# First unit's second maxima settled one step earlier, third unit's q and k projected later, in a fused attention kernel

## The chip, the cores and the metric

The kernel runs on one core of a Trainium2 chip. Such a core has a matrix engine (TensorE, PE in the profile; its weight loads are PEld), a vector engine (VectorE, DVE), an activation engine (ScalarE, ACT), a general engine (GpSimd, POOL) and a small engine that here only starts transfers (SyncE, SP). They run side by side and wait for one another through semaphores. Transfers run on 16 DMA engines. A time is the device time of one execution in microseconds; of several runs the median is given.

## The reference

A mixture-of-experts block, causal attention, and the same mixture-of-experts block again, each added to its input, for x of 8 batches x 1024 tokens x 256 features:

```python
x = x + 0.5 * _L0_ffn_ref(_layernorm(x), ...)
x = x + _L0_attn_ref(_layernorm(x), Wq, bq, Wkv, bkv, Wo, bo)
x = x + 0.5 * _L0_ffn_ref(_layernorm(x), ...)
...
dots = jnp.einsum('bhid,bhjd->bhij', q * scale, k)
dots = jnp.where(causal, MASK_VAL, dots)
attn = jax.nn.softmax(dots, axis=-1)
out = jnp.einsum('bhij,bhjd->bhid', attn, v)
```

There are 16 heads of 16 features. An expert that more than 1280 of the 16384 choices (two for each token) fall to is dropped with all its tokens. The kernel counts the choices and runs the expert code only if some expert stays under that bound; with these inputs only the attention and the two counts run.

## The kernel before

`attention` (L684) works in 32 **units**: a unit u is one batch (b = u // 4) and one group of four heads (g = u % 4). For a unit there are four kinds of work.

- **Projection**, `project(u)` (L821): two halves of 512 tokens. A half is 16 matmuls into a tile pq, a copy with bias into `packed` on ACT, and eight transfers of 32 KB (L845) that spread the heads over the rows of kT and qT, all on SP's queue except those of the first unit's k. kT and qT have four buffers each, used in turn.
- **Maxima**, `m_steps(u)` (L851): 24 steps of score blocks (tile `sm`) whose row maxima DVE takes, with the causal mask where it applies, into the columns of `top0` (queries 0 to 511) and `top1` (queries 512 to 1023).
- **Settling**, `settle(u, hf)` (L885): DVE turns `top` (a 32x32 transpose, tile `turned`), SP sends it to memory (L889, `top_d`), and three steps later fetches it back (L891) as a 17th row of each head of qT. The matching row of kT is -1, so that the scores of the next kind of work come out less their maximum.
- **Scores and values**, `e_steps(u)` (L897): 24 steps. Score blocks come out transposed (tile `sc`), ACT takes their exponential (`pT`), POOL masks the diagonal, and matmuls with v (`vaug`) add up in `pav`. Steps 0 to 7 are queries 0 to 511, steps 8 to 23 the others. The first sc of steps 8 on needs the row of `settle(u, 1)`.

The main loop (L1211) takes the scores and values of unit u together with the maxima of unit u + 1, step by step. It begins with u = -1, where only unit 0's maxima are there. From step 14 of u = -1 on, the first eight score steps of unit 0 run beside them. So in u = 0 steps 0 to 7 have maxima of unit 1 alone (in pairs, at even steps), and steps 8 to 23 have both.

The six score tiles (L698) take turns, `sm` and `sc` alike, and a second pool of two banks (L702) serves pq, pv, px, pav and the rest.

Everything else is fed in by a small planner, `Beside` (L53). A piece of work is a generator: it yields a number (go on in so many steps), PIECE or QK (go on when a step offers that kind), or REST (the second part of a piece just begun: it goes on in the next step). `step(kinds)` first runs all that is due by its number, then one piece of an offered kind. `finish` runs a work to its end at once. At the start of u = 0 the planner holds the values of batch 0's last tiles (`values_of`, tile pv), the remaining weight preparation (`turning`: pt_w, then g_mean and gcs on DVE, pt_gc, pg, pb_v), the residual of batch 0, `project(2)`, whose kind is QK, and `prepare(1, ...)` (L730), which loads batch 1 and later takes its layer-norm statistics, one tile of 128 tokens at a time, on DVE. `prepare` must be done by unit 1's step 7.

PE, DVE, ACT and POOL keep the order in which the program names their work; SP's order comes from the scheduler that builds the kernel.

All engine instructions go through one helper, so the profile shows line 37 for nearly all of them: tiles tell them apart. Transfers carry their own lines.

Of the kernel before, what the change touches and what calls it, by code (L numbers as in the profile page):

```python
# [49 lines left out]
PIECE, QK, REST = "piece", "qk", "rest"  # L50
# [53 lines left out]
def macaron_kernel(  # L104
# [210 lines left out]
    def ln_stats(xb, j, st, mv):  # L315
        vector.bn_stats(st[:, j, :], xb[:, j, :D])
        vector.bn_aggr(mv[:, j, :], st[:, j, :])

    def ln_tiles(what):
        st = norm.tile([P, TB, 6], F32, tag="st", name=f"st_{what}")  # L320
        mv = norm.tile([P, TB, 2], F32, tag="mv", name=f"mv_{what}")
        return st, mv

    def ln_rstd(mv, what, std=None):
        n = mv.shape[1]
        ve = norm.tile([P, TB], F32, tag="ve", name=f"ve_{what}")
        gpsimd.tensor_scalar(ve[:, :n], mv[:, :, 1], EPS, None, ALU.add)
        rstd = norm.tile([P, TB], F32, tag="rstd", name=f"rstd_{what}")
        gpsimd.tensor_tensor(rstd[:, :n], ve[:, :n], half[:, :n], ALU.pow)
        if std is not None:  # L330
            gpsimd.tensor_tensor(std, ve[:, :n], rstd[:, :n], ALU.mult)
        return rstd
# [351 lines left out]
    def attention(run_no, src, dst, gate0, logits, tally):  # L684
# [3 lines left out]
        with stack:  # L688
# [41 lines left out]
            def prepare(b, wait, apart):  # L730
                xb = xbs[b] = ap.tile([P, TB, D + E], F32, tag="xa", name=f"xa{b}", bufs=3)
                nc.sync.dma_start(out=xb[:, :, :D], in_=src[b].rearrange("(j p) d -> p j d", p=P))
                yield wait
                st, mv = ln_tiles(f"a{b}")
                for j in range(TB):
                    ln_stats(xb, j, st, mv)
                    yield apart
                stds[b] = norm.tile([P, TB], F32, tag="std", name=f"std{b}")
                lns[b] = mv, ln_rstd(mv, f"a{b}", stds[b])
                yield 2  # L740
# [62 lines left out]
            def residual(b):  # L803
                xb, lg = xbs[b], lgs.pop(b)
                gpsimd.tensor_tensor(
                    xb[:, :, D:], lg, stds.pop(b).unsqueeze(2).to_broadcast([P, TB, E]), ALU.mult
                )
                for j in range(0, TB, 2):
                    part = xb[:, j : j + 2, :]
                    gpsimd.tensor_tensor(part, part, bo_all.unsqueeze(1).to_broadcast([P, 2, D + E]), ALU.add)  # L810
                    yield 2
# [9 lines left out]
            def project(u, parts=(0, 512)):  # L821
                b, g = divmod(u, NG)
                xnT = xnTs[b]
                for s0 in parts:
                    yield QK
                    pq = bank(f"pq{u}_{s0}")
                    for c in range(DC):
                        matmul_cols(
                            pq,
                            wkqT[:, c, g].rearrange("p a d -> p (a d)"),  # L830
                            xnT[:, c, s0 : s0 + 512],
                            start=(c == 0),
                            stop=(c == DC - 1),
                        )
                        if c + 1 < DC:
                            yield REST
                    packed = ap.tile([P, 512], F32, tag="packed", name=f"packed{u}_{s0}", bufs=4)
                    scalar.activation(packed, pq, AF.Identity, bias=bkqT[:, g : g + 1], scale=1.0)
                    if u > 3:

                        nc.sync.dma_start(out=qTs[u % 4][HD::32, s0 : s0 + 512], in_=zeros)
                    for k in range(8):
                        r = 32 * (k % 4)

                        (nc.scalar if u == 0 and k < 4 else nc.sync).dma_start(  # L845
                            out=(kTs, qTs)[k // 4][u % 4][r : r + HD, s0 : s0 + 512],
                            in_=packed[HD * k : HD * (k + 1), :],
                        )
# [36 lines left out]
            def settle(u, hf):  # L885
                turned = ap.tile([P, 32], F32, tag="turned", name=f"turned{u}_{hf}")
                vector.transpose(turned, tops[hf])
                top_d = spill.tile([32, 4, 32], F32, tag="top_d", name=f"top_d{run_no}_{u}_{hf}", bufs=3)
                nc.sync.dma_start(out=top_d.rearrange("c b p -> b c p"), in_=turned)  # L889
                yield 3  # L890
                nc.sync.dma_start(  # L891
                    out=qTs[u % 4][HD::32, hf * 512 : hf * 512 + 512],
                    in_=top_d[:16].rearrange("(h i) b p -> h (i b p)", h=4),
                )
# [308 lines left out]
            beside = Beside()  # L1203
# [7 lines left out]
            for u in range(-1, NU):  # L1211
                b, g = divmod(u, NG)
                if u == 0:
                    beside.finish(opening)
                    preparing = beside.add(prepare(1, 2, 2))
                    projecting = beside.add(project(2))
                    beside.add(chain((PIECE,), turning, residual(0)))
                if u >= 0 and g == 2 and b + 1 < B:
# [9 lines left out]
                if g == 3 and u >= 0:  # L1228
                    if b + 2 < B:
                        preparing = beside.add(prepare(b + 2, STEPS + 8, 1))  # L1230
# [5 lines left out]
                def step(k, e):  # L1236


                    scores, then = es[e]
                    for h in range(2):  # L1240
                        scores(h)
                        if ms[k] is not None:
                            ms[k](h)
                    now = u * STEPS + k
                    if then is not None:
                        owed.append((now + 2, then, 0))
                        owed.append((now + 3, then, 1))
                    while owed and owed[0][0] <= now:
                        _, then, part = owed.popleft()
                        then(part)  # L1250
# [4 lines left out]
                for k in range(STEPS) if u < 0 else range(8) if u == 0 else ():  # L1255
                    if u < 0 and 14 <= k < 22:
                        step(k, k - 14)
                    elif k % 2 == 0:
                        for h in range(2):
                            ms[k](h)  # L1260
                            ms[k + 1](h)
                    if u < 0 and k == 7:
                        beside.add(settle(0, 0), first=True)
                        for kT in kTs[2:]:
                            scalar.copy(kT, row16.to_broadcast([P, S]))
                    if u == 0 and k == 1:
                        while owed:
                            _, then, part = owed.popleft()
                            then(part)
                        settling = beside.add(settle(0, 1), first=True)  # L1270
                    if u == 0 and k == 7:
                        beside.finish(settling)
                    beside.step((QK, PIECE) if u == 0 or not 14 <= k < 20 else ())
                for k in range(0, STEPS, 2) if u == NU - 1 else ():

                    then = es[k + 1][1]
# [21 lines left out]
                for k in range(0 if u else 8, STEPS) if 0 <= u < NU - 1 else ():  # L1298
# [30 lines left out]
                    if k == 0:  # L1329
                        settling = beside.add(settle(u, 1), first=True)  # L1330
# [30 lines left out]
    logits = [route.tile([P, NT, E], F32, name=f"logits{k}") for k in range(2)]  # L1361
    tallies = [tally_tile("0"), tally_tile("1")]
    leasts = attention(0, x, out, (logits[0], tallies[0]), logits[1], tallies[1])
    some0 = kept("0", leasts[0])
    either = route.tile([P, 1], I32, name="either")
    vector.scalar_tensor_tensor(either, leasts[1], float(CAP), some0, ALU.is_le, ALU.max)
    with tc.If(branch_on(either) > 0):
        some1 = kept("1", leasts[1])

        with tc.If(flag(some0, "0") > 0):  # L1370
            feed_forward(0, logits[0], x, xw_d)
            tally = tally_tile("1b")
            anew = attention(1, xw_d, out, None, logits[1], tally)
            vector.tensor_copy(some1, kept("1b", anew[1]))
        with tc.If(flag(some1, "1") > 0):
            feed_forward(1, logits[1], out, out)
# [40 lines left out]
```

## Time and profile before

| | us |
|---|---|
| median of 3 runs (lowest, highest) | 1357.85 (1356.86, 1359.06) |
| the profiled execution | 1351.15 |
| its span, first to last instruction | 1349.4 |
| idle time of TensorE before an `sc` that waited for qT<-top_d | 8.6 |
| mean granted TensorE clock, share of full | 0.989 |

Beside these, 40 equal slices of the span are shown on the page as digits: the busy tenths of each engine and the clock granted to TensorE.

```profile
PE   6799999999999999999999999999999999999994
PEld 2233333333333333333333333333333333333331
DVE  6766677778777787877778777777787777877865
...
PEclk9999999999999999999999999999999999999997
```

A slice is 33.7 us; the second one (33.7 to 67.5) is where the change is, and PE has a 7 there. A stall of some microseconds is visible only in a finer view: the list of waits (who waited, for whom, how long in total, how often, the longest), the chain of work that ended last with start times, the timeline of one engine, or the busy time of the engines in chosen stretches.

### The profile page before, as it was taken

The numbers are of one execution on the slowest core, as the hardware profiler recorded it, in microseconds if no ns is written. First come the engines' busy times: TensorE is split into PE (matmuls) and PEld (weight loads), VectorE is DVE, ScalarE is ACT, GpSimd is POOL, SyncE is SP. The second block draws the span as 40 slices with busy tenths as digits, with TensorE's granted clock in tenths as the row PEclk, the third lists the DMA queues.
The fourth block names the chain that finished last, engine by engine and source line by source line (L and its number), as shares of the span: only waits on it lengthen the run. The fifth ranks groups of instructions, "written<-read, shape, count | busy, mean of one in ns | idle before, by whom it ended". The sixth has DMA issues, their size and how long they took to land.

```text
span 1349.4 us, 51518 instructions
## 1 busy us (share of the span) xinstructions
PE 1309.2 (97%) x20664; PEld 436.6 (32%) x20664; DVE 1016.4 (75%) x3299; ACT 806.7 (60%) x1908; POOL 439.8 (33%) x776
## 2 busy tenths in 40 slices
PE   6799999999999999999999999999999999999994
PEld 2233333333333333333333333333333333333331
DVE  6766677778777787877778777777787777877865
ACT  3346666566666665666666666656566666666562
POOL 3134113542146221452125521354214621143321
PEclk9999999999999999999999999999999999999997
DMA  4101112112211121222122221211221111122201
GB/s 146 41 4 43 43 39 61 58 47 69 59 54 57 53 62 49 61 59 59 51 59 61 58 75 38 62 57 52 65 61 55 55 53 32 48 60 60 64 24 34
DMA packets 67024, 73.73 MB, mean 55 GB/s; under 512 B 24688, under 2 KB 42232, under 8 KB 66776
## 3 DMA queue, kind: packets, MB, share of 16 engines
q1 hardware_dynamic: 65432, 69.56, 17.7%
q8 instruction: 165, 2.70, 0.8%
q10 hardware_dynamic: 1344, 0.79, 0.2%
q14 instruction: 83, 0.68, 0.2%
HBM read 26.87 MB, written 26.20 MB: 39 GB/s over the span
## 4 chain that ended last, share of the span: by engine, by line
PE 94%; DVE 3%; DMA 1%; SPq 1%; issue 1%; ACT 0%; POOL 0%; ACTq 0%; DVEq 0%
PE sc L37 42%; PE pav L37 24%; PE pq L37 8%; PE sm L37 8%; PE pv L37 4%; PE px L37 4%; PE pta L37 1%; SPq L845 1%; DVE first L37 1%; DMA xa<-in_L_attn_x_dram 0%; PE px_last L37 0%; DVE st_g L37 0%; DVE cand_g L37 0%; DVE xa L37 0%; POOL rstd_g L37 0%
## 5 line engine op out<-in xcount | busy, mean ns | idle before, releaser
L37 ACT ACTIVATE pT<-sc 128x512 f32<-128x512 f32 (+3 forms) x1536 | 669.0, 488 | 469.8 <-PE sm L37 353.7
L37 PE MATMUL sm<-kT,qT 32*64 32x512 f32 (+3 forms) x6144 | 726.9, 507 | 0.0
L37 PE MATMUL sc<-qT,kT 32*64 32x512 f32 (+3 forms) x6144 | 695.1, 507 | 8.6 <-DMA qT<-top_d 8.6
L37 POOL TENSOR_SCALAR_AFFINE_SELECT pT<-pT 128x256 f32<-128x256 f32 x512 | 207.6, 407 | 772.6 <-ACT pT L37 765.0
L37 DVE TENSOR_REDUCE first<-sm 128x1 f32<-128x512 f32 x512 | 328.3, 684 | 82.2 <-PE sm L37 66.7
L37 PE MATMUL pav<-pT,vaug 128*32 128x160 f32 (+4 forms) x5120 | 381.9, 370 | 2.8 <-POOL pT L37 2.0
L37 DVE CUSTOM_DVE_ANT_0 sm<-sm,causal 128x256 f32<-128x256 f32 (+3 forms) x512 | 242.2, 516 | 117.9 <-PE sm L37 110.1
L37 DVE CUSTOM_DVE_ANT_0 sm<-sm,causal,first 128x256 f32<-128x256 f32 (+3 forms) x512 | 262.3, 557 | 86.1 <-PE sm L37 74.1
L37 PEld LDWEIGHTS sc<-qT,kT 32*64 32x64 f32 x6144 | 184.3, 130 | 376.9 <-ACT pT L37 303.7
L37 PEld LDWEIGHTS pav<-pT,vaug 128*32 128x32 f32 x5120 | 102.4, 108 | 363.1 <-issue 268.3
L37 PEld LDWEIGHTS sm<-kT,qT 32*64 32x64 f32 x6144 | 203.3, 130 | 14.2 <-issue 4.3
L37 DVE DVE_READ_ACCUMULATOR2_ANT top<- 128x1 f32 x1024 | 145.7, 142 | 0.0
L37 PE MATMUL pq<-xnT,wkqT 128*32 128x512 f32 x1024 | 135.2, 604 | 1.5 <-DVE xnT L37 0.8
L37 PE MATMUL pv<-wvT,xnT 128*32 128x264 f32 x1024 | 80.0, 389 | 1.1 <-ACT wvT L37 0.9
L37 PE MATMUL px<-woT,on 128*32 128x264 f32 x960 | 76.2, 389 | 0.2 <-DVE xa L37 0.2
L37 POOL TENSOR_SCALAR xn_a<-xa,mv_a,rstd_a 128x256 f32<-128x256 f32 x56 | 67.7, 1221 | 0.0
L37 POOL TENSOR_TENSOR xa<-row,xa 128x264 f32<-128x264 f32 x56 | 41.8, 746 | 50.4 <-ACT row L37 50.4
L37 ACT ACTIVATE packed<-pq,bkqT 128x512 f32<-128x512 f32 x64 | 45.4, 709 | 12.3 <-PE pq L37 8.8
L37 POOL TENSOR_TENSOR xa<-xa,bo_all 128x528 f32<-128x528 f32 x32 | 41.3, 1312 | 19.3 <-issue 18.8
L37 PEld LDWEIGHTS pq<-xnT,wkqT 128*32 128x32 f32 x1024 | 25.7, 110 | 55.9 <-issue 50.8
L37 POOL TENSOR_TENSOR on<-on,inv 128x512 f32<-128x512 f32 (+1 forms) x32 | 40.3, 1278 | 9.7 <-DMA inv<-inv_d 9.7
L37 PEld LDWEIGHTS pv<-wvT,xnT 128*32 128x32 f32 x1024 | 29.7, 109 | 26.1 <-ACT att L37 14.1
(125 smaller groups left out, 455.2 us busy)
## 6 DMA issues: line engine op xcount, KB each, us to landing
att_d<-att SPq DMA_DIRECT2D x62, 256.0 KB
qT<-packed SPq DMA_DIRECT2D x256, 32.0 KB
out_dram<-xa SPq DMA_DIRECT2D x16, 512.0 KB
kT<-packed SPq DMA_DIRECT2D x248, 32.0 KB
on<-att_d SPq DMA_DIRECT2D x30, 256.0 KB
inv<-inv_d SPq DMA_DIRECT2D x30, 256.0 KB
xa<-in_L_attn_x_dram SPq DMA_DIRECT2D x7, 1024.0 KB
xa<-in_L_attn_x_dram SPq DMA_DIRECT2D x2, 512.0 KB
```

Source lines behind the costliest of these rows:

```text
L37: i = call(*args, **kwargs)
L845: (nc.scalar if u == 0 and k < 4 else nc.sync).dma_start(out=(kTs, qTs)[k // 4][u % 4][r : r + HD, s0 : s0 + 512], in_=packed[HD * k : HD ...
```

## The change

Four places change, all in the part of the main loop for u = -1 and u = 0.

- `settle(0, 1)` is added at the last step of u = -1 (step 23) instead of at step 1 of u = 0. It is finished by step 4 of u = 0 instead of step 7.
- In steps 0 to 7 of u = 0 the planner is offered PIECE alone; before, QK came first. `project(2)` is therefore taken from step 8 on, where the offer (PIECE, QK) is as it was.
- `prepare(1, ...)` begins its statistics 10 steps after its load is issued instead of 2, and takes one tile in every step instead of in every second one.

```diff
                     beside.finish(opening)
-                    preparing = beside.add(prepare(1, 2, 2))
+                    preparing = beside.add(prepare(1, 10, 1))
                     projecting = beside.add(project(2))
...
                             scalar.copy(kT, row16.to_broadcast([P, S]))
+                    if u < 0 and k == 23:
+                        settling = beside.add(settle(0, 1), first=True)
                     if u == 0 and k == 1:
                         while owed:
                             _, then, part = owed.popleft()
                             then(part)
-                        settling = beside.add(settle(0, 1), first=True)
-                    if u == 0 and k == 7:
+                    if u == 0 and k == 4:
                         beside.finish(settling)
-                    beside.step((QK, PIECE) if u == 0 or not 14 <= k < 20 else ())
+
+                    beside.step((PIECE,) if u == 0 else (QK, PIECE) if not 14 <= k < 20 else ())
```

In the built kernel the number of instructions is the same. What moves on each engine: on DVE the turn of `top1` goes ahead of unit 1's first four blocks, and the eight statistics pairs, three of which lay between unit 1's first blocks, all lie behind its blocks of step 10 to step 17. On PE the two projections (pq, 16 matmuls each) go from steps 1 to 3 of u = 0 to steps 9 to 12, each in two halves, and pv, pt_w, pt_gc, pg and pb_v move up, pt_gc and pg ahead of step 8. On SP the fetch of unit 0's second maxima goes from behind unit 2's sixteen transfers to right behind its own send; unit 2's transfers now come after unit 1's first settling. On ACT the copies to `packed` go along with their projections. On POOL the four additions of the residual now come in one row.

## The prediction

> **What bounds the kernel now.** I read the page from the top: the span and the busy shares, the chain of work that ended last, then who waited for whom.
>
> ```profile
> span 1349.4 us, 51518 instructions
> ...
> PE 1309.2 (97%) x20664; PEld 436.6 (32%) x20664; DVE 1016.4 (75%) x3299; ACT 806.7 (60%) x1908; POOL 439.8 (33%) x776
> ...
> PE 94%; DVE 3%; DMA 1%; SPq 1%; issue 1%; ACT 0%; POOL 0%; ACTq 0%; DVEq 0%
> ```
>
> TensorE (PE) is busy 97% of the span and makes 94% of the chain. So only time in which PE stands, or runs slow, can be won. The list of waits has one long stand of PE that happens once:
>
> ```profile
> PE sc L37 <- DMA qT<-top_d: 8.6, 1, 8.6
> ```
>
> The chain of waits between 45 and 80 us says where it comes from (start, us, what):
>
> ```profile
> 54.81 0.08 DVE turned L37
> 54.90 0.57 SPq L889
> ...
> 66.44 0.59 SPq L845
> 67.02 0.05 issue
> 67.12 1.81 DMA qT<-top_d
> 68.93 0.14 issue
> 69.06 1.12 PE sc L37 x2
> ```
>
> The second-half maxima of unit 0 are turned at 54.8 and sent to memory at 54.9, but the transfer that brings them back as a row of qT is issued only at 67.12. SP's own timeline shows what lies between:
>
> ```profile
> 56.08 3.35 SPq L845 DMA_DIRECT2D kT<-packed  x4
> 59.53 2.44 SPq L845 DMA_DIRECT2D qT<-packed  x4
> 62.07 2.43 SPq L845 DMA_DIRECT2D kT<-packed  x4
> 64.54 2.48 SPq L845 DMA_DIRECT2D qT<-packed  x4
> 67.12 0.53 SPq L891 DMA_DIRECT2D qT<-top_d  x1
> ```
>
> Sixteen issues for unit 2 stand ahead of one row that PE wants now. PE finished its last work (pt_w, 59.78 + 0.66) at 60.43 and stands to 69.06: 8.63 us. It then starts at half clock. In the windows below the columns are stretch, its us, PE busy, PEld, DVE, ACT, POOL, granted clock, DMA:
>
> ```profile
> 22.04:25.45 3.41, 2.50 (x39) 1.22 (x38) 3.41 (x13) 0.66 (x2) 0.00 (x0) 1.00 0.34 76
> 59.60:63.01 3.41, 0.84 (x12) 0.42 (x4) 2.22 (x13) 1.03 (x3) 0.29 (x1) 1.00 0.23 51
> 69.84:73.25 3.41, 3.41 (x32) 1.50 (x16) 1.93 (x5) 1.28 (x3) 0.00 (x0) 0.50 0.00 0
> 1322.50:1325.95 3.45, 1.76 (x16) 0.58 (x16) 2.62 (x13) 0.93 (x6) 2.18 (x6) 1.00 0.24 81
> ```
>
> The clock falls to 0.50 at about 63.0 and returns at 73.24. From restart to unit 1's first sc (97.77) PE takes 28.71 us. Taking out pt_gc 0.21, pg 1.44 and pb_v 1.09 leaves 25.97. The same steps at full clock: steps 11 to 23 take 97.77 - 76.37 - 1.09 (pb_v) = 20.31, steps 8 to 10 1.04 each (88.02 to 89.06 for one sc/sm group): 23.4 in all. So the slow restart costs 2.5 us, and **11.2 us** stand to be won here.
>
> **Settle moved to the end of unit -1.** In the built order of the changed kernel the turn follows unit 0's last maximum directly on DVE (ends 50.98), ahead of the four 512-wide blocks that held it until 54.67. Its 0.21 us hide in DVE's wait for PE (52.11). top_d is issued near 51.25; the two other settles of this stretch issue the return 2.03 us after top_d (74.57 to 76.60), and it lands 1.94 us after its issue (67.12 to 69.06): the row is there at **55.3**. On SP both issues are now ahead of att_d and all of unit 2's. SP waits about 1.4 us for top_d meanwhile; att_d behind it is needed much later. So this wait goes entirely, PE getting there later than 55.3.
>
> **What is late next: gcs.** In the new PE order pt_gc and pg come before the first sc of step 8. pt_gc needs gcs, from DVE, which was busy without a gap here:
>
> ```profile
> 58.57 0.47 DVE L37 CUSTOM_DVE_ANT_0 sm<-sm,causal 128x256 f32<-128x256 f32 x1
> ...
> 61.00 0.37 DVE L37 TENSOR_REDUCE g_mean<-gsb 8x1 f32<-8x256 f32 x1
> ```
>
> New DVE order: four 512-wide blocks, 52.11 to 54.67; four 384-wide, 2.03 (54.90 to 56.93), to 56.70; four 256-wide, 1.47 (57.48 to 58.95), to 58.17; g_mean to gcs 0.93 (61.00 to 61.93), to **59.10**; the 128-wide blocks after. PE's own work is done by about 57.8. pt_gc 59.15, its copy on ACT 0.17 (59.46 to 59.63), pg 59.7 plus 1.44: the first sc at **61.1** instead of 69.06, with pt_gc and pg behind it already.
>
> **Unit 2's q and k from step 8.** 16 pq matmuls take 1.85 us on PE (35.15), twice: 3.70. They were at 52 to 56.7 in the cover of DVE's backlog; now they lie on the path and count in full. Their two packed copies (0.69 each) fit beside the exponentials, 1.08 in a step of 1.45 or more. Their 16 issues, some 0.62 each, run from about 69 to 80; unit 2 is first read at about 91, so 9 us or more cover them. top_d of unit 1 goes ahead of them on SP, and its next one is due at unit 1.
>
> **Statistics from step 10, one tile a step.** Eight pairs at 0.55 (56.93 to 57.48), 4.4 us on DVE either way. Three leave the stretch before gcs (counted above) and all lie in steps 10 to 17. There DVE has two reductions 1.21 (83.36 to 84.57) plus 0.55 = 1.76 a step, 1.89 in steps 16 and 17; PE has 1.04 + pav 0.41 or 0.73 = 1.45 or 1.77, and in steps 9 to 12 0.93 of pq more. From step 13 DVE is over PE by 0.31, 0, 0.31, 0.12, 0.44: 1.2 us. Six score tiles let PE run ahead of part of it. Between 0 and 1.2 without hand-over gaps; I take 0.5. rstd on POOL follows near step 18, as before, needed at unit 1's step 7. bo_all is there earlier, so POOL's four residual additions (1.31 each) end before step 16 wants POOL.
>
> **The clock, rule against row.** PE now stands about 0.9 + 1.3 + 0.3 us between 56.5 and 59.7, with under 0.7 of work between. [...] The rows are stricter: of windows that long, one 25% busy and one 51% busy were followed by half clock, one 73% busy was not. Wherever a window falls over 56.5 to 61.1, one has at most some 55% busy. I go by the rows: one window of 3.41 at half clock costs 1.7, with the ramp **2.0**. A second such window makes 3.7; the low end is 0.3.
>
> **The sum.** Restart 61.1 + steps 23.4 + pb_v 1.1 + pq 3.7 = 89.3 against 97.77: 8.5. Less 2.0 and 0.5: **6.0 us**. Everything behind unit 0 keeps its order and moves along. The profiled execution took 1351.15 (1.75 around its span): it would take 1345.1. The timed runs stand 6.7 higher, spread 2.2, for a reason the trace doesn't show; I take the same 6.0 off their median: 1357.85 - 6.0 = **1351.9**.
>
> **Rivals.**
> [...]
> - A, DVE takes over as the bound. The gaps before DVE's reductions were 0.23 to 0.64 between 75 and 85; if each of steps 12 to 17 adds 0.3 to the 1.2, it costs 3.0, and with two cold windows 8.5 - 3.7 - 3.0 = 1.8: 1356.0. For: DVE was near full there with five tiles. Against: PE got a longer stretch too (19 us for 17.4 of DVE).
> - C, **slower**: half clock holds on through steps 8 to 23, because PE waits for DVE each step and no window is full enough. Each window costs 1.7; from the fifth (17 us) the 8.5 are gone. Eight windows: 1357.9 + 5.6 = 1363.4. Against: one full window, 69.84 to 73.25, restored it.
> - D, the change doesn't do what it says: the row comes ahead but unit 2's transfers, moved 14 us later, arrive after 91 and give the stand back: nothing, 1357.9. Against: 9 us of cover.
>
> **How the numbers follow.** Forecast 0.62, B 0.20, A 0.09, C 0.05, D 0.04. About 0.2%, 2.7 us, is what the measurement tells from no change. Faster takes forecast and B, 0.82; same A and D, 0.13; slower C, 0.05. The bounds give gains of 8.2 (0.3, 0) to 3.6 (3.7, 1.2); with B and A in, and about 1 us for the spread of the runs, 1348.5 to 1356.2.
>
> **What would show it.** Right: no wait of PE for qT<-top_d; L891 about 2 us after L889 near 51; pt_gc near 59.2, waiting for gcs; first sc of step 8 near 61; unit 1's first sc near 92; the granted clock under 1.00 for one window near 60 to 64. DVE's idle gone in steps 13 to 17. Wrong: PE standing before unit 2's first sm; clock at 0.50 beyond 66; pq behind a free bank.

## The result, and the profile after

| | before | after |
|---|---|---|
| median of 12 runs (lowest, highest), us | 1356.71 (1351.99, 1359.06) | 1346.91 (1345.34, 1352.08) |
| ratio of times, 95% interval | | 0.9936 [0.9921, 0.9951] |
| the profiled execution, us | 1351.15 | 1345.34 |
| its span, us; mean granted clock | 1349.4; 0.989 | 1343.5; 0.992 |

The changed kernel is faster, by 9.8 us between the medians, against 6.0 foretold; 1346.91 lies 1.6 us below the range. Yet the two profiled executions differ by 5.8 us, almost exactly the sum that the prediction made for them (1345.1 foretold, 1345.34 measured). So the profile was read rightly on the whole, and something is different between the profiled execution of before and most of its others.

First the page of after: span, busy time of the engines, and the chain that ended last.

```profile
span 1343.5 us, 51517 instructions
...
PE 1310.3 (98%) x20664; PEld 436.0 (32%) x20664; DVE 1016.6 (76%) x3299; ACT 806.8 (60%) x1908; POOL 439.8 (33%) x776
...
PE 94%; DVE 3%; DMA 1%; issue 1%; ACT 0%; ACTq 0%; POOL 0%; DVEq 0%
```

TensorE works as long as before (1310.3 against 1309.2 us) in a shorter span, and SP's queue is gone from the chain. SP's timeline of after shows why (start, us, line of the transfer):

```profile
52.02 0.57 SPq L889 DMA_DIRECT2D top_d<-turned  x1
54.03 0.50 SPq L891 DMA_DIRECT2D qT<-top_d  x1
...
70.50 0.50 SPq L891 DMA_DIRECT2D qT<-top_d  x1
71.09 3.49 SPq L845 DMA_DIRECT2D kT<-packed  x4
```

The row is fetched 2.01 us behind its send, and unit 2's sixteen transfers begin at 71.09, behind unit 1's first settling. PE's timeline of after shows what is late instead (in brackets: idle time before it, and for whom it waited):

```profile
60.07 0.26 PE L37 MATMUL pt_gc<-ident,gcs 8*128 8x8 f32 x2 [1.23 <-DVE gcs L37]
60.68 0.58 PE L37 MATMUL pg<-gcT,bo_cols 128*128 128x8 f32 x4 [0.35 <-ACT gcT L37]
...
62.09 0.93 PE L37 MATMUL sc<-qT,kT 32*64 32x512 f32 x2
```

PE waits 1.23 us for gcs and 0.35 for its turned copy; the first sc of step 8 starts without a wait of its own. The same execution in windows, stretches of 3.41 us counted from the changes of the granted clock, which stood at 0.50 for just one of them here (columns: stretch, us, busy time of PE, PEld, DVE, ACT, POOL, granted clock, DMA):

```profile
58.91:62.32 3.41, 1.90 (x22) 1.84 (x30) 1.95 (x13) 0.30 (x3) 0.00 (x0) 1.00 0.00 0
62.32:65.74 3.42, 3.42 (x20) 1.17 (x4) 1.29 (x2) 1.20 (x4) 0.00 (x0) 0.50 0.02 5
65.74:69.15 3.41, 3.41 (x45) 0.78 (x48) 1.90 (x5) 1.15 (x3) 2.56 (x3) 1.00 0.01 5
```

A window in which PE was 56% busy is followed by one at half clock, and by no more. Unit 1's first sc comes at 92.04 us, against 97.77 before. The two executions differ by 0.7 us already ahead of the change: the last `pv` that both orders have in common starts at 50.56 us, against 49.85. Counted from there, the way to unit 1's first sc is 6.4 us shorter (41.48 instead of 47.92).

### The profile page after: what moved, and what is told of

It reads as the page before. It is cut to its first block, busy times and chain, and to the rows that moved or that the text cites. A ratio compares the mean times of both kernels' runs of the same rounds, so it can differ in the third digit from the quotient of the medians.

```text
span 1343.5 us, 51517 instructions
## 1 busy us (share of the span) xinstructions
PE 1310.3 (98%) x20664; PEld 436.0 (32%) x20664; DVE 1016.6 (76%) x3299; ACT 806.8 (60%) x1908; POOL 439.8 (33%) x776
## 4 chain that ended last, share of the span: by engine, by line
PE 94%; DVE 3%; DMA 1%; issue 1%; ACT 0%; ACTq 0%; POOL 0%; DVEq 0%
PE sc L37 43%; PE pav L37 24%; PE pq L37 9%; PE sm L37 8%; PE pv L37 4%; PE px L37 4%; PE pta L37 1%; DVE first L37 1%; ACTq L845 0%; DMA xa<-in_L_attn_x_dram 0%; DVE sm L37 0%; PE px_last L37 0%; DVE st_g L37 0%; DVE xa L37 0%; DVE cand_g L37 0%
```

## Experiments

Medians are in us. A kernel is compared with those that ran on the same chip, and by its ratio to the kernel before, which ran beside each of them. That last common pv starts between 49.28 and 51.57 us in the profiles, so distances are counted from its start where a tenth of a microsecond matters.

### Where the other 4 us are: both kernels once more

> The kernel before, once more, to see what its spread (1351.2 to 1359.1) is made of: each run comes with its span and its mean granted clock. Theory 1 (clock): the long stand of TensorE is followed by a varying stretch at half clock; runs near 1357 then show a mean clock some 0.004 to 0.007 under the 0.989 of the run profiled first (5 to 9 us lost are 10 to 19 us at half clock), and a profile of such a run shows half clock well beyond 73 us. Theory 2 (transfers): the stand itself is longer, about 14 us instead of 8.6; the clock differs by at most 0.003. Theory 3 (elsewhere): the extra time lies outside 50 to 100 us, at the start or the end, and the changed kernel has it too.

> The changed kernel, once more, on the same chip as the other runs of this call. Theory 1 and 2: spread of 1345 to 1349, gain over the kernel before 8 to 10 us in the median, 5.9 between the quickest of each. Theory 3: the same two groups of times as the kernel before, and a median gain of 6.

Measured: the kernel before 1358.02 (1352.04 to 1360.08, 21 runs), ratio to itself 0.9997 [0.9985, 1.0009]; the changed kernel 1346.93 (1345.55 to 1349.44, 5 runs), ratio 0.9914 [0.9901, 0.9928].

Each run comes with its mean granted clock, and that tells it. Of the 46 runs of the kernel before on this chip, 36 have a mean clock of 0.982 to 0.985 and took 1356.02 to 1360.24 (median 1358.4); 10 have 0.988 to 0.991 and took 1351.46 to 1354.60 (median 1353.2). Nothing lies between on this chip; on two others 12 of 82 runs do, at 0.986 or 0.987. (The mean counts the end of the kernel too, where the clock is at half for 20 us in the first profile of before and 18 in that of after, so it is a rough sign.) The execution profiled at first, 1351.15 at 0.989, was one of the few; the one profiled now, 1357.89 at 0.985, is one of the many, though 29 of those 36 have a mean a little lower still, which no profile explains. In windows of that length:

```profile
68.68:72.09 3.41, 2.07 (x20) 1.31 (x24) 0.00 (x0) 0.01 (x1) 0.00 (x0) 0.50 0.02 5
72.09:75.49 3.40, 3.40 (x31) 1.11 (x28) 3.00 (x6) 2.34 (x5) 0.00 (x0) 0.50 0.00 0
75.49:78.90 3.41, 3.41 (x25) 1.86 (x9) 1.92 (x6) 1.08 (x2) 0.00 (x0) 0.50 0.03 5
78.90:82.31 3.41, 3.41 (x29) 1.31 (x28) 0.65 (x2) 0.77 (x4) 0.00 (x0) 0.50 0.03 7
82.31:85.71 3.40, 3.40 (x24) 1.51 (x20) 1.19 (x3) 0.55 (x2) 0.59 (x1) 0.50 0.00 0
85.71:89.12 3.41, 3.41 (x54) 1.18 (x48) 2.88 (x6) 2.17 (x4) 3.25 (x3) 1.00 0.01 2
```

The first of the expectation's three theories came true. The stand is the same (8.73 us, first sc of step 8 at 70.02). But the clock stays at 0.50 through four windows in which PE is busy to the full, and comes back at 85.71; in the execution profiled first, one full window was enough. From restart to unit 1's first sc (103.93) it takes 33.91 us instead of 28.71. By the prediction's own working (23.4 for the steps and 2.74 for pt_gc, pg and pb_v at full clock) the slow restart costs 33.91 - 26.14 = **7.8 us** here, not 2.5. From the last common pv to unit 1's first sc this execution takes 53.23 us and the first one 47.92; the difference in this stretch, 5.3 us, is that of the two restarts (33.91 - 28.71 = 5.2) to a tenth.

### The parts of the change, alone

`settle_only`, on the kernel before:

```diff
+                    if u < 0 and k == 23:
+                        settling = beside.add(settle(0, 1), first=True)
...
-                        settling = beside.add(settle(0, 1), first=True)
-                    if u == 0 and k == 7:
+                    if u == 0 and k == 4:
```

> Only the settling of unit 0's second maxima is moved; projection of unit 2 and statistics stay where they were before. If the row's way through SP is the whole cause (my working): no wait for qT<-top_d, pq back in the cover of DVE's backlog, the first sc of step 8 near 60 to 61 at full clock, unit 1 some 5 us earlier than in the changed kernel: 1341 to 1343, 14 to 15 us under the kernel before. If moving the projection is needed (rival: unit 2's issues still get ahead of the row, or DVE's backlog with three statistics more becomes the bound): 1347 or more.

`qk_only`, on the kernel before:

```diff
-                    beside.step((QK, PIECE) if u == 0 or not 14 <= k < 20 else ())
+                    beside.step((PIECE,) if u == 0 else (QK, PIECE) if not 14 <= k < 20 else ())
```

> Only unit 2's projection is moved behind step 8; the settling stays at step 1 of unit 0, the statistics where they were. The sixteen issues are gone from between send and fetch, so the row is asked for about 2 us after its send at 54.9 and lands near 59; TensorE gets to pt_gc when gcs is there, with three statistics (1.65 us) and the turn in front of it, near 61. By my working 1 to 2.5 us slower than the changed kernel: 1348 to 1350. Rival: the settling's own place matters (the row still late): 1352 or more.

`no_qk`, the changed kernel with that line as it was (settling and statistics moved, the projection not):

```diff
-                    beside.step((PIECE,) if u == 0 else (QK, PIECE) if not 14 <= k < 20 else ())
+                    beside.step((QK, PIECE) if u == 0 or not 14 <= k < 20 else ())
```

> The changed kernel with unit 2's projection back in steps 1 to 3 of unit 0: settling moved and statistics from step 10. Against the kernel with only the settling moved (1343.8) it tells what the statistics are worth. My working: three statistics (1.65 us) leave the stretch where DVE is behind, and none is paid later: 1342 to 1343.5. Rival: DVE becomes the bound in steps 13 to 17: 1344.5 to 1346.

`stats_back`, the changed kernel with the statistics where they were:

```diff
-                    preparing = beside.add(prepare(1, 10, 1))
+                    preparing = beside.add(prepare(1, 2, 2))
```

> The changed kernel with the statistics where they were (from step 2, every second step). The settling is moved, the projection too. Three statistics (1.65 us) are again ahead of gcs, for which pt_gc waits: by my working 1.1 to 1.6 us slower than the changed kernel, whose own clock loss stays: 1347.5 to 1349. Rival: DVE in steps 13 to 17 had cost as much as it gave: 1346 to 1347.

| | median (lowest, highest; runs) | ratio to before [95%] | half clock between 56 and 100 us, profiled | unit 1's first sc | the same from the last common pv |
|---|---|---|---|---|---|
| before_again | 1358.02 (1352.04, 1360.08; 21) | 0.9997 [0.9985, 1.0009] | 20.5 | 103.93 | 53.23 |
| qk_only | 1349.22 (1347.44, 1350.61; 5) | 0.9928 [0.9914, 0.9942] | 6.8 | 95.50 | 43.93 |
| after_again | 1346.93 (1345.55, 1349.44; 5) | 0.9914 [0.9901, 0.9928] | 6.8 | 93.48 | 43.00 |
| settle_only | 1343.83 (1341.51, 1344.72; 4) | 0.9887 [0.9872, 0.9902] | none | 89.90 | 38.98 |
| no_qk (another chip) | 1342.54 (1341.62, 1345.01; 6) | 0.9908 [0.9887, 0.9928] | none | 89.34 | 38.46 |
| stats_back (a third chip) | 1349.34 (1348.45, 1350.33; 6) | 0.9935 [0.9916, 0.9953] | 6.8 | 95.41 | 44.01 |

qk_only and no_qk came as expected; settle_only is 0.8 and stats_back 0.3 us above its range. Moving the settling is what brings the gain, 14.2 us by itself; the last column has 14.2 as well (53.23 - 38.98). Moving the projection takes the sixteen transfers from in front of the fetch too, so alone it also ends the long stand (8.8 us); but on top of the settling it makes things worse: the changed kernel, which moves projection and statistics as well, is 3.1 us slower than settle_only on the same chip, and none of their runs overlap. Why, shows in no_qk in stretches of 10 us:

```profile
50.00:60.00 10.00, 9.83 (x164) 3.21 (x160) 8.18 (x36) 3.28 (x9) 0.81 (x3) 1.00 0.18 50
60.00:70.00 10.00, 10.00 (x126) 4.43 (x121) 7.92 (x25) 5.67 (x14) 0.29 (x1) 1.00 0.19 41
```

With the projection at its old place PE has work while DVE catches up, goes over into step 8 (first sc at 60.79) without standing, and pt_gc and pg fall behind it, where gcs has long been there. The clock doesn't drop in this stretch. All runs of no_qk (1341.62 to 1345.01) are under all of the changed kernel, but on another chip, and the intervals of the two ratios overlap; its profile says so more clearly, 38.46 us against 41.48 and 43.00. Between no_qk and settle_only the ratios tell no difference.

The statistics matter through gcs, by about 1 us. In stats_back, PE's timeline:

```profile
61.93 0.26 PE L37 MATMUL pt_gc<-ident,gcs 8*128 8x8 f32 x2 [1.76 <-DVE gcs L37]
```

Two pairs, not the three expected, are back ahead of gcs on DVE (58.28 and 60.30; the third follows at 62.67). pt_gc comes 1.9 us later than in the profile of the changed kernel that also has two slow windows (after_again, 60.00), but 0.9 of that is there already ahead of the change (last common pv at 51.40 instead of 50.48). That leaves 1.0 for the statistics, beside 1.1 of work for two pairs, and 1.0 at unit 1's first sc (44.01 against 43.00). The ratios of whole runs don't tell it from the noise (0.9935 against 0.9914 and 0.9936, on three chips). What the statistics cost in steps 10 to 17 doesn't show on PE: in after it is busy for 10.00 of the 10 us from 70 and from 80.

### The stand given back to the changed kernel

`stand_kept` and `stand_long` add idle transfers of zeros between send and fetch of unit 0's second maxima, 26 and 46 of them:

```diff
                 yield 3
-                nc.sync.dma_start(
+                for n in range(26) if (u, hf) == (0, 1) else ():
+                    d = nc.sync.dma_start(out=idle_d[n], in_=zeros)
...
+                d = nc.sync.dma_start(
                     out=qTs[u % 4][HD::32, hf * 512 : hf * 512 + 512],
```

> The changed kernel with 26 idle transfers of 8 KB put on SP between send and fetch of unit 0's second maxima, so that the row lands near 70 us and TensorE stands about 8.5 us ahead of step 8 as in the kernel before, but with pb_v and unit 2's projection behind the stand. Cost of the stand alone: 8.5 us over the changed kernel, 1354 to 1356. Theory H2: pb_v and pq bring the clock back within one or two windows in all runs: 1353 to 1357, clock 0.986 to 0.990, one group. Theory H3 (the length of the stand alone decides how long half clock holds): half clock for some 20 us in most runs, 1360 or more, clock 0.984 or less.

> As the kernel with 26 idle transfers, which were issued every 0.34 us rather than 0.6 so that the row landed at 64 and the stand came to only 0.56 us; now 46, so that the row lands near 71 and TensorE stands some 8 us behind pg. The stand itself then costs about 7 us over the 1350 of that kernel, for pg at half clock is hidden in it, less what half clock before the stand had cost: 1355 to 1358. If pg ahead of the stand and pq behind step 9 let the clock return within two windows: clock 0.986 or more in nearly all runs. If pb_v alone is enough to hold half clock: a second group 5 us or more higher, clock 0.984 or less.

stand_kept: 1350.07 (1348.42 to 1355.32, 18 runs), 0.9955 [0.9944, 0.9966]. It missed its aim: an idle transfer takes 0.34 us of SP (6.74 for 20), where one of unit 2's takes some 0.62 (2.48 for 4 in the first profile of before), so the stand was only 0.56 us.

stand_long: 1355.74 (1353.85 to 1357.69, 22 runs), 0.9988 [0.9977, 0.9998]. SP's and PE's timelines:

```profile
55.82 13.86 SPq L894 DMA_DIRECT2D idle_d<-zeros  x40
69.78 0.53 SPq L897 DMA_DIRECT2D qT<-top_d  x1
```

```profile
61.63 1.82 PE L37 MATMUL pg<-gcT,wsb 128*128 128x8 f32 x8
71.70 1.11 PE L37 MATMUL sc<-qT,kT 32*64 32x512 f32 x2 [8.25 <-DMA qT<-top_d]
```

With a stand of 8.25 us nearly the whole gain is gone: the fetch's place on SP is the cause. Its restart is 9.6 us later than that of after (0.5 of it from a later start), and from there to unit 1's first sc (101.77) it takes 30.07 us, as in after (29.95). So in this execution, with pg done ahead, the long stand cost itself and one slow window. 19 of the 22 runs have a mean clock of 0.986 to 0.989; the three at 0.983 or 0.984 were not profiled. What makes the restart of the kernel before cost 7.8 is to be looked for in what runs behind it.

### gcs ahead

`gcs_early`, the changed kernel with the five lines that make g_mean and gcs two pieces earlier:

```diff
+        mean = const.tile([E, 1], F32, name="g_mean")
+        vector.tensor_reduce(mean, gsb, AX.X, ALU.add)
...
         turn(wvs, wvT[:, :, :D])
         yield PIECE
```

> The changed kernel with the three small DVE operations that make gcs moved ahead, into unit -1, so that pt_gc waits for nothing. By my working TensorE gets to the first sc of step 8 about 1.3 us earlier; its stand before is then about 0.9 us of the wait for score tiles. If the stand of 1.2 + 0.35 us is what drops the clock: no half clock, 1343 to 1344.5, clock 0.993. Rival: the window is still too empty (pg counts little): half clock as before, 1345.5 to 1346.

1345.39 (1343.55 to 1346.20, 6 runs), 0.9925 [0.9905, 0.9944]. The rival came: pt_gc no longer waits for gcs, but the clock drops all the same. In windows:

```profile
58.11:61.53 3.42, 3.07 (x36) 2.04 (x34) 1.72 (x12) 0.50 (x4) 0.00 (x0) 0.99 0.03 5
61.53:64.95 3.42, 3.42 (x28) 1.50 (x20) 1.72 (x3) 1.08 (x2) 0.53 (x1) 0.51 0.00 0
```

A window that is 90% busy was followed by half clock. It is the one with pt_gc and pg in it (58.49 to 60.6).

### What holds the half clock

`turning_late`, the kernel before with the preparation of the output weights, pg among it, held back by 16 steps:

```diff
-                    beside.add(chain((PIECE,), turning, residual(0)))
+                    beside.add(chain((PIECE, 16), turning, residual(0)))
```

> The kernel before, with pt_w, pt_gc, pg and pb_v moved 16 steps back, out of the stretch that follows the stand: there is only sc, sm and pav behind it; the stand of 8.7 us stays. Most runs of the kernel before (36 of 46) kept half clock to about 85 us, 10 of 46 to about 73. Theory H1 (the small-N, weight-load matmuls of pg and pb_v keep a window from counting as busy): without them the clock returns after the first whole window in all runs; 1350 to 1353, clock 0.988 or more, no second group. Theory H2 (blocks of 32 rows, sc and sm, hardly count; whole-array work brings the clock back): without pb_v and pq the return is as late or later; 1357 to 1360, clock 0.985 or less.

1354.26 (1351.80 to 1356.67, 22 runs), 0.9982 [0.9972, 0.9991]. The stand is there in full (8.93 us), but the group of runs at 0.982 to 0.985 is gone: all 22 have 0.986 to 0.989, where 27 of the 39 runs of the kernel before on this chip have 0.985 or less. That is what H1 said of the groups; the time is 1.3 us above its range, and the profile shows a slow window that H1 didn't have, behind pg at its new place:

```profile
103.43:106.84 3.41, 3.41 (x52) 2.13 (x44) 1.86 (x8) 1.72 (x7) 0.81 (x2) 0.99 0.36 117
106.84:110.25 3.41, 3.41 (x44) 0.74 (x32) 1.40 (x7) 1.19 (x4) 0.41 (x1) 0.50 0.21 45
```

pg runs there from 104.96 to 106.47, in a window that PE fills.

`turning_late_idle` adds idle matmuls of pg's and pb_v's forms to it, after steps 10 and 11:

```diff
+                    if u == 0 and k == 10:
+                        idle = bank("idle_pg")
+                        for _ in range(6):
+                            matmul(idle[:, :E], ident, iota_e)
+                    if u == 0 and k == 11:
...
```

> The kernel with the weight preparation moved 16 steps back (1351.8 to 1356.7, clock 0.986 to 0.989 in 22 runs), and in its old place idle matmuls of the same shapes whose result nobody reads: six of 128x128 by 8 columns after step 10, two of 128x128 by 264 columns after step 11. Their own work is about 2.5 us at full clock (pg 1.44, pb_v 1.09 before). Theory H1 (such matmuls keep windows from counting as busy): the group with long half clock comes back, some runs at 1358 or more with a clock of 0.985 or less. Rival (where the weight preparation sits has another effect, for instance through DVE): one group, 1354 to 1359, clock not under 0.986.

1355.77 (1353.95 to 1359.67, 22 runs), 0.9993 [0.9982, 1.0003]. This tells nothing for or against: 2 of 22 runs are at 0.985 or less, and in the profiled one the clock was back at 74.5, before the first idle matmul (75.48).

What the profiles so far have in common is this: every full window at half clock between 60 and 86 us with pt_gc or pg in it was followed by another at half clock, and the first full one without them by full clock (before_again: pt_gc at 74.80, pg from 77.04 to 79.77, full clock from 85.71; after_again: pg from 60.61 to 63.26, full clock from 67.49; qk_only: pg from 62.77 to 65.46, full clock from 69.19). Both are matmuls of 8 columns; in the first profile of before each of pg's is listed with 0.26 us, and a weight load of 0.19 us beside it. Two kernels put this to the test, turning_late with idle matmuls in every step right behind the restart, narrow ones in `idle_small`, wide ones of about the same time in `idle_wide`:

```diff
+                    if u == 0 and 8 <= k <= 12:
+                        idle = bank("idle")
+                        for n in range(6):
+                            matmul(idle[:, :E], (ident, causal[:, :P])[n % 2], iota_e)
```

```diff
+                        for n in range(3):
+                            matmul(idle[:, :240], (ident, causal[:, :P])[n % 2], causal[:, :240])
```

> This is the kernel before with the preparation of the output weights (pt_w, gcs, pt_gc, pg, pb_v) held back by 16 steps, as in turning_late, and six idle matmuls with 8 columns (12 records, the form of pg) after each of steps 8 to 12 of unit 0, right behind the stand of 8.9 us. Their own time at full clock is 5 x 1.50 = 7.5 us. Theory: a window in which matmuls of 8 columns run does not bring the clock back, however busy TensorE is. Then half clock holds until the last group has run: five steps at half clock with 2.66 us of idle matmuls each, some 24 us from the restart near 70, so to about 94 and the end of that window, 26 to 31 us of half clock in all, a mean clock of 0.978 to 0.981, and 1354.3 + 7.5 + 8 to 10 = 1370 to 1372 us. Rival: what counts is only that TensorE is busy; then the first full window after the restart brings the clock back as in turning_late, 10 to 14 us of half clock, mean clock 0.986 to 0.989, and 1354.3 + 7.5 to 8.5 = 1362 to 1363.

> As idle_small, with three idle matmuls of 240 columns (6 records, the form of pb_v, worked out from its row: 1.58 us at full clock) in place of the six of 8 columns after each of the five steps: 7.9 us of idle work. Theory and rival agree here: no matmul of 8 columns runs, the first full window after the restart brings the clock back, 10 to 14 us of half clock, mean clock 0.986 to 0.989, and 1354.3 + 7.9 to 9 = 1362 to 1363 us. If this kernel too holds half clock for 25 us, extra work of any kind keeps it, and the theory of the 8 columns falls.

idle_small: 1370.97 (1370.38 to 1371.93, 4 runs), 1.0103 [1.0080, 1.0126], mean clock 0.979 to 0.980. Windows behind the restart and at the end, and its last idle matmuls:

```profile
71.87:75.28 3.41, 3.41 (x28) 2.91 (x28) 1.81 (x4) 1.08 (x2) 0.00 (x0) 0.50 0.00 0
75.28:78.69 3.41, 3.41 (x25) 1.80 (x17) 1.41 (x3) 1.08 (x2) 0.00 (x0) 0.50 0.00 0
...
92.35:95.76 3.41, 3.41 (x24) 2.96 (x28) 1.03 (x3) 0.31 (x1) 0.00 (x0) 0.50 0.00 0
95.76:99.15 3.39, 3.39 (x40) 0.68 (x25) 1.29 (x2) 1.08 (x2) 0.00 (x0) 0.51 0.00 0
99.17:102.58 3.41, 3.41 (x60) 1.11 (x48) 2.81 (x6) 2.10 (x4) 0.00 (x0) 1.00 0.00 0
```

```profile
94.93 0.57 PE L37 MATMUL idle<-iota_e,causal 128*128 128x8 f32 x2
```

PE is busy to the full from 71.87 on, and the clock stays at half until the first whole window behind the last narrow matmul, 34.1 us in all, some 3 to 8 more than expected, with time and mean clock as expected. Even the window with 0.63 us of narrow matmuls in it (88.93 to 92.35, the last of them over at 89.56) was followed by half clock. idle_wide: 1360.87 (1357.87 to 1362.20, 14 runs; 1.1 below its range), 1.0030 [1.0020, 1.0040], clock 0.986 to 0.990:

```profile
68.72:72.13 3.41, 3.41 (x20) 1.63 (x21) 1.40 (x3) 1.08 (x2) 0.00 (x0) 0.51 0.00 0
72.13:75.54 3.41, 3.41 (x34) 1.88 (x40) 1.82 (x5) 1.08 (x2) 0.00 (x0) 1.00 0.00 0
```

With wide matmuls in it, from 70.77 on (1.36 us of the window), the first full window brings the clock back, and no run of the 14 has a mean clock near the four of idle_small. So of two kernels with about the same stand (9.22 and 9.32 us) and about as much extra work behind it, the one with matmuls of 8 columns had 34.1 us of half clock, and the one with 240 columns had full clock again at 72.13. What of the form makes the difference, the 8 columns or the weight loads beside them (2.91 us of the window from 71.87 in idle_small, 1.63 of the one from 68.72 in idle_wide), these two kernels don't separate.

## Why the prediction was right about the profile and wrong about the time

- **The stand and where it goes**: as worked out. It is gone, SP's order is the cause (stand_long), the fetch follows its send by 2.01 us. The row's way took the time that was read from unit 1's settles (2.01 us against 2.03 from send to fetch).
- **What is late next, gcs**: right, and right in size. pt_gc 60.07 and first sc 62.09 stand 0.9 to 1.0 behind the forecast; 0.7 of that is there already ahead of the change (the last common pv starts at 50.56 instead of 49.85).
- **Projection in full on the path**: pq x8 takes 1.00, 1.00, 0.86 and 0.86 in the chain of after, 3.72 against 3.70. That it also uncovers the wait for gcs was in the forecast, but not as a cost of this part: leaving it where it was (no_qk) brings unit 1's first sc 3.0 us closer to the last common pv than in after and 4.5 closer than in after_again.
- **Statistics 0.5**: from 62.09 to 92.04 are 29.95 us; 23.4 + 1.1 + 3.7 and one slow window (1.7) make 29.9. Nothing is left for them. So part of the exact hit of the profile is luck: PE reached step 8 later than foretold by 1.0, and the 0.5 and the ramp of 0.3 did not come.
- **The clock, 2.0 for one new window**: one window of 3.42 us in the execution profiled first, two in the second: within its bounds (0.3 to 3.7), though half clock beyond 66 us, named as a sign of being wrong, came in the second (to 67.49). Going by the rows gave the right sign, in part by luck, for the busy share alone doesn't tell which windows are followed by half clock (last section): a window 56% busy was (after, from 58.91), and so was one 90% busy with pg in it (gcs_early, from 58.11). No run shows the ramp of 0.3, a loss of its own at PE's restart, that is in the 2.0 and is the low end of the range: the 29.95 us of after are made up without it (the point above).
- **The step that failed: "So the slow restart costs 2.5 us", and with it "I take the same 6.0 off their median"**. The 2.5 was measured in an execution of the smaller group, where one window restored the clock. In a profile of the larger group it is 7.8. The 6.7 us by which the timed runs stood above the profiled execution, left "for a reason the trace doesn't show", were mainly these 5.3 us. With 7.8 the same sum gives a gain of 11.3; measured were 11.1 on one chip and 9.8 in the result, where 4 of the 12 runs of before have times like those of the smaller group (1351.99 to 1353.19). The time that follows, 1357.85 - 11.3 = 1346.6 against 1346.91, is closer than the sum deserves: it leaves out the second slow window that the changed kernel had in after_again.
- **Rivals**: what C feared, half clock holding on through windows that PE fills, was seen (before_again, 72.09 to 85.71), but in the kernel before, where it argued for the change. What spoke against C, that one full window restored the clock, did not hold in the other profile of before. A, B and D did not come: DVE did not become the bound (PE was busy for all of the time from 70 to 90), the clock fell to 0.50 (62.32), and the last of unit 2's transfers was issued by 82.2, 10 us ahead of their use.

**What decides the two groups.** In the two profiles, the first full window after the restart either lies before the step with pt_gc and pg, or reaches into it. Half clock lasted 3.41 us in after, 6.83 in after_again, 10.24 in the first profile of before, 20.5 in before_again and 34.1 in idle_small, all near whole multiples of 3.41, and where it began differs by more than the kernel's own shift (62.98 in the first profile of before and 65.23 in before_again, with the last matmul ahead of the stand over at 60.43 and 61.29). Counted in windows from there, in the first profile one began at 69.83, 0.8 us behind the restart, and was over (73.24) before pt_gc (73.61); in before_again the first whole one began at 72.09, 2.1 us behind the restart, and had pt_gc in it. In the changed kernel pg is ahead of step 8, and its two profiles lose one window and two; 16 of its 17 runs have mean clocks of 0.988 to 0.993, and one, 1352.08 us at 0.985, lost more for a reason that no profile shows. That the phase of the windows makes the choice is read from two profiles; no run set the phase. An estimate from them: pt_gc comes 4.6 to 4.8 us behind the restart, so a window of 3.41 fits ahead of it if it begins in the first 1.1 to 1.4 us, which is one case in three for a random phase; 10 of 46 runs were of the quicker group on this chip. How little of a narrow matmul it takes isn't settled either: pt_gc's two records last 0.38 us.

## What to carry to other kernels

Before a gain is taken off a median, set the profiled execution beside all runs: if their mean clocks fall into two groups, profile one of each, and value the stall in the group that makes the median. Look at where preparatory matmuls of few columns lie: in this kernel half clock lasted 20.5 us (before_again) and 34.1 us (idle_small) with matmuls of 8 columns in the windows behind a stand of 8.7 and 9.2 us, and none to three windows where pt_gc and pg lay elsewhere (none in no_qk and settle_only, three in stand_kept). Try putting a transfer that the bound engine waits for ahead of bulk transfers on its queue, and leaving the work that covered the wait where it was: here that gave 14.2 us (settle_only), and 11.1 with projection and statistics moved as well.

## What the runs showed of the hardware that was not expected

- TensorE busy to the full by the trace went with a granted clock of 0.50 as well as 1.00. With matmuls of 128 x 128 weights and 8 columns in its work it stayed at half clock for 27 gapless us (idle_small, 71.87 to 99.15); with matmuls of 240 columns full clock came back at 72.13, after one full window (idle_wide).
- At full clock the same matmuls went either way. The window from 73.24 to 76.65 in the first profile of before has pt_gc and all of pg in it and was followed by full clock; the one from 103.43 to 106.84 in turning_late, busy to the full as well with pg in it, was followed by half clock. What decides between them is open.
- The busy share alone decided neither way. At full clock, a window 90% busy was followed by half clock (gcs_early from 58.11), two of 69% and 73% were not (the first profile of before from 15.21 and from 22.03). At half clock, three windows busy to the full did not bring the clock back (before_again from 72.09 to 82.31), one 87% busy did (the first profile of before from 1329.34).
- A transfer of zeros of 8 KB to memory took SP 0.34 us to issue (stand_kept, 6.74 for 20), one of the same core's 32 KB transfers of packed rows 0.62 (before, 2.48 for 4): places in this queue were not alike in time.
